# Cross-attention on one core: first context tile in pieces, one DMA request per weight chunk, another written-out order

## The chip, the core and the metric

The kernel runs on one NeuronCore of a Trainium2 chip. Five engines work side by side, each from its own queue in order: TensorE (PE in the profile, with its weight loads as PEld), VectorE (DVE), ScalarE (ACT), GpSimd (POOL) and SyncE (SP), which here only issues DMA requests. Sixteen DMA engines move the data. The metric is the device time of one execution in microseconds (us).

## The reference

Everything is float32. 64 batches of text rows (256 x 512) attend to context rows (256 x 384); hidden size 512:

```python
text_p  = x   @ W_text  + b_text        # (64, 256, 512) @ (512, 512)
audio_p = ctx @ W_audio + b_audio       # (64, 256, 384) @ (384, 512)
Q = layer_norm(text_p,  g1, beta1)
K = layer_norm(audio_p, g2, beta2)
alpha = softmax(Q @ K.T / sqrt(512))
h = alpha @ audio_p                     # V is audio_p
out = layer_norm(h @ W_out + b_out + x, g_out, beta_out)
```

## The kernel before, in words

**Algebra.** The kernel folds W_audio and W_out into one matrix (`fold_multiply`, `wao_sb`), so that the context is weighted directly (`context_*`, `z_part`) and multiplied once. The large products are done by fast schemes that trade multiplications for additions: the projection of q (`Fork`) and the scores take seven block products instead of eight, the projection of k and the output product (`Thirds`) fifteen instead of eighteen. The additions are spread over DVE, POOL and ACT.

**Order.** Nothing is scheduled by a tool while the kernel is built: each engine executes its instructions in the order in which the text calls the methods, and semaphores make a consumer wait for its producer. After the methods' definitions the text has three stretches: first rounds (batches 0 to 2 are started, weights are prepared), a loop `for b in range(3, B - 3)` of 58 rounds in which five batches are in different stages at once (`q2`, `k2` projected, `at` scored, `last` weighted, `old` multiplied out, `settled` normalised), and an end, in which the last batches run out. In each stretch the calls are written in an order worked out by hand or by a planner; the same call set could stand in another order.

**Transfers at the start.** Loads are issued mostly from SP's queue, two early ones from ACT's. A weight matrix lies in SBUF with its rows dealt out in squares: partition q·32 + i holds row (q, k, i) of chunk k. `weight_chunks(t, w, lo, n, queues)` loads chunks lo to lo + n - 1 with four requests, one for each q, each to 32 partitions. The order on SP's queue: the two tiles of the first context batch `c_0`; chunk 0 of the audio weight `wa` (alternating between ACT and SP); chunks 1 and 2 of it; the two tiles of `x_0`; chunks 0 and 1 of the text weight `wt`; the bias row `ba`; chunks 2 and 3 of `wt`; then the second batch's context `cq_1` (`load_c`, four requests by squares, as `load_x`), `bt`, `xq_1`, the output weight `wo`, a bias, and five small requests for `vectors` (`load_vectors`, L163).

**First products.** `keep_busy(6)` runs matmuls on a tile of ones that nothing reads (L187). `RowTurn.tile(t)` turns a tile of batch 0: DVE copies it into squares (`arrange`, L179), PE transposes it chunk by chunk (L202), ACT copies the result out of PSUM (L203). `Projection.multiply(t, chunks)` (L440) then multiplies turned rows by weight chunks: `k[0]` by `wa`, `q[0]` by `wt`, `k[1]` by the centred `wa`. `turn_weights` transposes weight squares (L215); `fold_multiply` (L244) needs `wo`. `means` and `centre` (L272, L279) take the mean off the weights, after which the row means of the projections vanish.

**In the loop.** The output product of a batch, `y`, is a `Thirds`: `y.one()` on PE, `y.copy_n1()` on ACT (L594), `y.start_t()` on DVE (L541), then `y.three()` on PE, which adds to what `start_t` wrote. `Fork.seed()` (ACT) puts the bias where `q3.one()` adds its product. The weights of a batch's softmax go through DRAM to be turned: `at.store_e()`, in the next round `last.fetch_e()`, then `last.turn_e()` on DVE (L76).

**At the end** the last batch's second tile is finished in halves, with two stores of 256 KB at the very end (`store`, L1369, and `store_beside`, L1334).

Of the kernel before, what the change touches and what calls it, by code (L numbers as in the profile page):

```python
# [22 lines left out]
def kernel(  # L23
# [87 lines left out]
    nc.gpsimd.memset(ones, 1.0)  # L111
# [24 lines left out]
    def weight_chunks(t, w, lo, n, queues):  # L136
        v = w.rearrange("(q k i) h -> q i k h", q=NQ, i=SQ)
        for q in range(NQ):
            queues[q].dma_start(t[q * SQ : (q + 1) * SQ, lo : lo + n], v[q, :, lo : lo + n])

    for t in range(ST):
        nc.sync.dma_start(c_0[:, t, :], c_first[:, t, :])
    weight_chunks(wa_sb, w_audio, 0, 1, [nc.scalar, nc.sync, nc.scalar, nc.sync])
    weight_chunks(wa_sb, w_audio, 1, 2, [nc.sync] * NQ)
    for t in range(LT):
        nc.sync.dma_start(x_0[:, t, :], x_first[:, t, :])
# [42 lines left out]
    class RowTurn:  # L189
# [6 lines left out]

        def tile(self, t):
            ar = self.ar[:, t]
            arrange(ar, self.rows[:, t, :], self.chunks, nc.vector.tensor_copy)
            ps = p_at.tile([P, self.chunks, P], F32, tag="at", name="ps_rows")  # L200
            for j in range(self.chunks):
                nc.tensor.transpose(ps[:, j, :], ar[:, j, :], ident)  # L202
            nc.scalar.copy(self.T[:, :, bass.ts(t, P)], ps)  # L203
# [1195 lines left out]

    keep_busy(6)  # L1400
    war = []
    bt_row = bt_sb.rearrange('p (o h) -> p o h', o=1)
    c_turn = RowTurn(c_0, AC, 'cT')
    var_0 = small.tile([P, 4], F32, tag='var4', name='var')
    wa_t = const.tile([P, 11, WP], F32, tag='wa_thirds', name='wa_thirds')
    wao_room = const.tile([P, HC * H], F32, tag='wo', name='wao_thirds')
    pool, tag = (once, 'e')
    c_turn.tile(0)
    k[0] = Projection('k', 0, c_turn.T, wa_sb, ba_sb, AC, ST, bank[0:2])
    war.append(pool.tile([P, HC, P], F32, tag=tag, name=f'war_{0}'))  # L1410
    x_turn = RowTurn(x_0, DC, 'xT')
    c_turn.tile(1)
    k[0].multiply(0, [0])
    pool, tag = (work, 'eT')
    k[0].multiply(1, [0])
    arrange(war[0], wa_sb[:, 0, :], HC, nc.gpsimd.tensor_copy)
    q[0] = Projection('q', 0, x_turn.T, wt_sb, bt_sb, DC, LT, bank[2:4])
    war.append(pool.tile([P, HC, P], F32, tag=tag, name=f'war_{1}'))
    arrange(war[1], wa_sb[:, 1, :], HC, nc.gpsimd.tensor_copy)
    k[0].multiply(1, [1])  # L1420
    mean_wa = means(wa_sb, AC, 'mwa')
    pool, tag = (work, 'eT')
    war.append(pool.tile([P, HC, P], F32, tag=tag, name=f'war_{2}'))
    k[0].multiply(0, [1])
    k[0].multiply(1, [2])
    arrange(war[2], wa_sb[:, 2, :], HC, nc.gpsimd.tensor_copy)
    x_turn.tile(0)
    ba_row = ba_sb.rearrange('p (o h) -> p o h', o=1)
    x_turn.tile(1)
    k[0].multiply(0, [2])  # L1430
    turn_weights(0, 1)
    q[0].multiply(1, [0])
    q[0].multiply(1, [1])
    centre(wa_sb, mean_wa, AC)
    mean_wt = means(wt_sb, DC, 'mwt')
    mean_ba = means(ba_row, 1, 'mba')
    q[0].multiply(0, [0])
    k[0].evict(1)
    k[0].evict(0)
    third_weights(wa_sb, wa_t, [0])  # L1440
    k[0].scales()
    k[0].normalise([1])
    q[0].multiply(0, [1])
    bt_step = const.tile([P, H2], F32, tag='bt_step', name='bt_step')
    mean_bt = means(bt_row, 1, 'mbt')
    cT[1] = turn_c(1)
    k[0].normalise([0])
    q[0].multiply(0, [2])
    q[0].multiply(0, [3])
    turn_weights(1, 1)  # L1450
    turn_weights(2, 1)
    k[1] = Projection('k', 1, cT.pop(1), wa_sb, ba_sb, AC, ST, bank[4:6])
    q[0].multiply(1, [2])
    k[1].multiply(1, [0])
    centre(ba_row, mean_ba, 1)
    k[1].multiply(0, [0])
    turn_weights(3, 1)
    k[1].multiply(1, [1])
    third_weights(wa_sb, wa_t, [2], nc.vector)
    xT[1] = turn_x(1)  # L1460
    q[0].multiply(1, [3])
    k[1].multiply(1, [2])
    k[1].multiply(0, [1])
    k[1].multiply(0, [2])
    fold_multiply(1, 0, 1)
    xs_1 = SumX(xT.pop(1), nc.vector)
    centre(wt_sb, mean_wt, DC)
    centre(bt_row, mean_bt, 1)
    q[0].evict(1)
    g1_sb, be1_sb, g2_sb, be2_sb, bac_sb = take_columns()  # L1470
    wa_blocks = third_weights(wa_sb, wa_t, [3])
    q[0].evict(0)
    wt_blocks = weight_sums(wt_sb, DC // 2, 'wtsum')
    fold_multiply(1, 1, 2)
    k[0].store()
    xs_1.add(1)
    xs_1.add(1)
    load_c(2)
    folds.append(p_at.tile([P, H], F32, tag='at', name='ps_fold'))
    xs[1] = xs_1  # L1480
    k[1].evict(1)
    q[1] = Fork(1, xs.pop(1).of, wt_blocks)
    load_x(2)
    k[1].evict(0)
    xs_1.add(1)
    fold_multiply(1, 2, 3)
    q[0].scales()
    fold_multiply(0, 0, 1)
    third_weights(wa_sb, wa_t, [1], nc.vector)
    part = bias_parts()  # L1490
    load_c(3)
    cT[2] = turn_c(2)
    Fork.seed()
    cs[2] = Sides(cT.pop(2), 'csum')
    q[0].normalise([0])
    cs[2].add(1)
    fold_multiply(2, 0, 1)
    q[1].seven()
    cs[2].add(1)
    cs[2].add(1)  # L1500
    q[1].one()
    nc.vector.tensor_tensor(bt_step, bt_sb[:, :H2], bt_sb[:, H2:], ALU.subtract)
    nc.vector.tensor_scalar(g2_sb, g2_sb, scale, None, ALU.mult)
    q[1].after_seven()
    xT[2] = turn_x(2)
    k[0].fetch()
    q[0].normalise([1])
    nc.vector.tensor_scalar(be2_sb, be2_sb, scale, None, ALU.mult)
    xs[2] = SumX(xT.pop(2))
    xs_1.add(1)  # L1510
    q[0].store()
    fold_multiply(0, 1, 2)
    fold_multiply(0, 2, 3)
    q[1].after_one()
    k[1].square()
    k[1].scales()
    q[1].six()
    q[1].start_q3()
    fold_multiply(0, 3, 4)
    q[1].step_r()  # L1520
    fold_evict(0)
# [3 lines left out]
    load_x(3)  # L1525
    Thirds.seed_with(ba_sb)
    cT[3] = turn_c(3)
    xs[2].add(1)
    cs[2].add(1)
    load_c(4)  # L1530
    bias_rest(part, 1, 2)
    fold_multiply(1, 3, 4)
    xs[2].add(1)
    ba_delta = third_bias(ba_sb, 'ba_delta')
    cs[3] = Sides(cT.pop(3), 'csum')
    k2_0 = k[2] = Thirds('k', 2, cs.pop(2), wa_blocks, ba_sb, ba_delta)
    q[0].fetch()
    q[1].five()
    k2_0.one()
    fold_evict(1)  # L1540
    q[1].after_five()
    xs[2].add(1)
    at_0 = att[0] = Attention(0)
    xs[2].add(1)
    cs[3].add(1)
    k2_0.copy_n1()
    q[2] = Fork(2, xs.pop(2).of, wt_blocks)
    k[1].normalise([0])
    k2_0.two()
    k[1].normalise([1])  # L1550
    at_0.k.turn()
    cs[3].add(1)
    q[1].two()
    third_weights(wa_sb, wa_t, [4], nc.vector)
    q[1].three()
    k2_0.start_t()
    cs[3].add(1)
    q[1].four()
    xT[3] = turn_x(3)
    q[1].square()  # L1560
    k[1].store()
    q[1].scales()
    fold_multiply(2, 1, 2)
    k2_0.three()
    k2_0.copy_t()
    var_2 = small.tile([P, 4], F32, tag='var4', name='var')
    fold_multiply(2, 2, 3)
    q2_0 = q[2]
    k2_0.start_l0()
    k2_0.start_l1()  # L1570
    cs[3].add(1)
    q[1].normalise([0])
    q[1].normalise([1])
    bias_rest(part, 2, 3)
    fold_multiply(2, 3, 4)
    q[1].store()
    cs[3].add(1)
    k2_0.four()
    Fork.seed()
    xs[3] = SumX(xT.pop(3))  # L1580
    cs[3].add(1)
    at_0.affine_keys(0)
    q2_0.one()
    k2_0.take_m()
    bias_rest(part, 3, 4)
    k2_0.start_u()
    q2_0.seven()
    q2_0.after_one()
    xs[3].add(1)
    fold_evict(2)  # L1590
    at_0.affine_keys(3)
    at_0.q.turn()
    load_c_rows(1)
    q2_0.six()
    q2_0.after_seven()
    q2_0.start_q3()
    load_x(4)
    k2_0.five()
    at_0.affine_queries(3)
    xs[3].add(1)  # L1600
    at_0.affine_queries(0)
    q[1].fetch()
    cs[3].add(1)
    k2_1 = k[3] = Thirds('k', 3, cs.pop(3), wa_blocks, ba_sb, ba_delta)
    last_1 = att[0]
    xs[3].add(1)
    k2_0.copy_n()
    k2_0.copy_u()
    xs[3].add(1)
    q[3] = Fork(3, xs.pop(3).of, wt_blocks)  # L1610
    q2_0.step_r()
    q2_0.five()
    k2_0.leave_middle()
    wao_t = wao_room[:, :11 * WP].rearrange('p (n h) -> p n h', n=11)
    at_0.affine_keys(2)
    at_0.affine_keys(1)
    k2_0.middle_d()
    k2_0.leave()
    q2_0.after_five()
    q2_1 = q[3]  # L1620
    fold_bias(part)
    k2_0.square(var_0[:, 2:], [0])
    at_0.score(0, 1)
    k2_0.leave_ends()
    at_0.affine_queries(2)
    q2_0.three()
    at_0.affine_queries(1)
    k2_0.middle_sum()
    k2_0.square(var_0[:, 2:], [1])
    third_weights(wao_sb, wao_t, [1])  # L1630
    q2_0.two()
    k2_0.seed()
    k[1].fetch()
    q2_0.four()
    at_0.score(1, 2)
    load_c(5)
    at_0.score(2, 3)
    q2_0.square(var_0[:, :2], [0])
    at_0.score(3, 4)
    cT[4] = turn_c(4)  # L1640
    q2_0.square(var_0[:, :2], [1])
    var_1 = small.tile([P, 4], F32, tag='var4', name='var')
    xT[4] = turn_x(4)
    scales_of(q2_0, k2_0, var_0)
    at_0.score(4, 5)
    cs[4] = Sides(cT.pop(4), 'csum')
# [829 lines left out]
```

## Time and profile before

| | |
|---|---|
| median of 3 runs | 1337.42 us (1336.81 to 1337.81) |
| profiled execution | 1338.2 us, its span 1336.0 us |
| PE busy | 1328.3 us, 99% of the span, 8495 instructions |
| DVE, ACT, POOL busy | 93%, 87%, 86% |
| granted PE clock | 1.000 |
| DMA queues | q1 (SP) 320.20 MB, 85.8% of 16 engines; q10 (ACT) 0.13 MB |
| HBM | 203.57 MB read, 116.65 MB written |

The span runs from the first to the last instruction of the profiled execution; times in the views are microseconds from the span's start. A busy share is that of one engine over the whole span; a matmul's end is modelled, so that starts of successive matmuls say more than its busy time. In the chain of waits each piece is what released the next one; a row of the timeline gives start, length, engine, line of the kernel, operation, written and read tile, and, in brackets, the idle time before it and who ended it. `x8` behind a row merges eight instructions; a float32 matmul of the text is two PE instructions.

### The profile page before, as it was taken

Reading aid. Unit: us, or ns where it says so; the run is one execution under the profiler, and the core shown is the slowest. Engines: PE = TensorE matmul, PEld = TensorE weight load, DVE = VectorE, ACT = ScalarE, POOL = GpSimd, SP = SyncE. Lnnn points to the kernel's source line nnn. Section 1 sums busy time; section 2 is a strip of 40 time slices with the busy share of each in tenths; the row PEclk is TensorE's granted clock in tenths of the full one; section 3 lists DMA queues with packets and bytes.
Section 4 is the critical chain, followed back from the end, with each engine's and each line's share of the span. In section 5 each row is a group of like instructions: output and inputs, shape, how many; then the busy total and the mean of one; then the engine's idle time right before and its main releaser. Section 6 shows DMA issues by size and latency. Waiting matters only on the chain.

```text
span 1336.0 us, 29959 instructions
## 1 busy us (share of the span) xinstructions
PE 1328.3 (99%) x8495; PEld 1249.6 (94%) x8495; DVE 1243.0 (93%) x3313; ACT 1162.9 (87%) x3310; POOL 1151.5 (86%) x1855
## 2 busy tenths in 40 slices
PE   9999999999999999999999999999999999999998
PEld 5899999999999999999999999999999999999996
DVE  6769999999999999999999999999999999999968
ACT  4898898898898898988988988988889889889885
POOL 5798898898898898988988988988989889889865
PEclk9999999999999999999999999999999999999999
DMA  9988989888888889889888898889988998888773
GB/s 220 243 235 236 242 246 246 242 255 240 251 251 247 245 247 240 259 244 238 255 234 242 253 243 247 243 230 266 254 235 251 255 240 252 246 244 253 209 229 138
DMA packets 448971, 322.24 MB, mean 241 GB/s; under 512 B 153765, under 2 KB 381349, under 8 KB 448806
## 3 DMA queue, kind: packets, MB, share of 16 engines
q1 hardware_dynamic: 448710, 320.20, 85.8%
q8 instruction: 68, 1.11, 0.4%
q14 instruction: 97, 0.79, 0.2%
q10 hardware_dynamic: 96, 0.13, 0.0%
HBM read 203.57 MB, written 116.65 MB: 240 GB/s over the span
## 4 chain that ended last, share of the span: by engine, by line
PE 98%; DMA 1%; ACT 1%; SPq 0%; DVE 0%; issue 0%; DVEq 0%; ACTq 0%
PE ps_f L733 28%; PE ps_m L557 16%; PE ps_sc L884 13%; PE ps_n L557 11%; PE ps_u L557 8%; PE ps_z L1033 7%; PE ps_l L557 5%; PE ps_z L1095 5%; PE ps_sc L823 1%; DMA eq<-ed 1%; PE ps_f L440 0%; PE ps_n L440 0%; PE ps_l L244 0%; PE ps_fold L244 0%; PE ps_u L440 0%; PE ps_m L244 0%
## 5 line engine op out<-in xcount | busy, mean ns | idle before, releaser
L869 POOL TENSOR_TENSOR qsum<-qT 128x256 f32<-128x256 f32 x118 | 112.5, 953 | 101.4 <-ACT qT L527 96.9
L352 POOL TENSOR_TENSOR csum<-csum,cT 128x256 f32<-128x256 f32 x310 | 194.0, 627 | 5.2
L733 PE MATMUL ps_f<-wtsum,xsum 128*128 128x256 f32 x756 | 194.0, 380 | 0.0
L527 ACT ACTIVATE qT<-qT,columns 128x256 f32<-128x256 f32 x256 | 152.2, 597 | 1.8 <-DVE qT L76 1.8
L733 PEld LDWEIGHTS ps_f<-wtsum,xsum 128*128 128x128 f32 x756 | 131.9, 191 | 11.4 <-issue 1.0
L527 ACT ACTIVATE kT<-kT,columns 128x256 f32<-128x256 f32 x256 | 141.2, 609 | 0.0
L733 PE MATMUL ps_f<-wt,xT 128*128 128x256 f32 x504 | 129.5, 379 | 0.0
L884 PE MATMUL ps_sc<-kT,qT 128*128 128x128 f32 x928 | 122.4, 275 | 0.0
L884 PEld LDWEIGHTS ps_sc<-kT,qT 128*128 128x128 f32 x928 | 114.8, 192 | 0.0
L884 PE MATMUL ps_sc<-ksum,qsum 128*128 128x128 f32 x696 | 106.2, 275 | 0.9 <-DVE ps_sc L541 0.9
L1357 DVE SCALAR_TENSOR_TENSOR yr<-yr,rstd,beo 128x512 f32<-128x512 f32 x120 | 106.6, 889 | 0.1
L884 PEld LDWEIGHTS ps_sc<-ksum,qsum 128*128 128x128 f32 x696 | 97.7, 191 | 5.0 <-DVE ps_sc L541 2.2
L733 PEld LDWEIGHTS ps_f<-wt,xT 128*128 128x128 f32 x504 | 91.0, 191 | 9.7
L1348 DVE SCALAR_TENSOR_TENSOR yr<-yr,nm,go 128x512 f32<-128x512 f32 x124 | 95.9, 774 | 0.0
L488 ACT ACTIVATE kr<-kr,rstd 128x512 f32<-128x512 f32 x126 | 92.7, 738 | 0.0
L314 POOL TENSOR_TENSOR xsum<-xT 128x256 f32<-128x256 f32 x124 | 90.6, 732 | 1.9 <-DVE xT L76 1.9
L541 DVE TENSOR_TENSOR ps_l<-ps_m,t 128x171 f32<-128x171 f32 x248 | 83.5, 337 | 7.8 <-ACT t L605 3.3
L1158 ACT ACTIVATE junk<-yr,nm 128x512 f32<-128x512 f32 x124 | 90.2, 727 | 0.3
L794 ACT ACTIVATE junk<-ps_f 128x512 f32<-128x512 f32 x126 | 75.2, 597 | 15.6 <-PE ps_f L733 13.5
L520 DVE STREAM_TRANSPOSE kT<-kq 128x512 f32<-128x512 f32 x122 | 85.3, 701 | 2.9 <-DMA kq<-kd 2.8
L804 ACT ACTIVATE qr<-ps_f,rstd 128x512 f32<-128x512 f32 x126 | 87.8, 699 | 0.1
L1095 PE MATMUL ps_z<-eT,c 128*128 128x256 f32 x296 | 84.6, 380 | 0.0
(302 smaller groups left out, 4653.7 us busy)
## 6 DMA issues: line engine op xcount, KB each, us to landing
kd<-kr SPq DMA_DIRECT2D x64, 512.0 KB, 2.9
kq<-kd SPq DMA_DIRECT2D x256, 128.0 KB, 3.1
qd<-qr SPq DMA_DIRECT2D x64, 512.0 KB, 2.8
qq<-qd SPq DMA_DIRECT2D x256, 128.0 KB, 2.8
xq<-in_x_dram SPq DMA_DIRECT2D x252, 128.0 KB, 3.1
x<-in_x_dram SPq DMA_DIRECT2D x63, 512.0 KB, 5.3
out_dram<-yr SPq DMA_DIRECT2D x62, 512.0 KB, 5.1
cq<-in_ctx_dram SPq DMA_DIRECT2D x252, 96.0 KB, 4.0
```

Source lines behind the costliest of these rows:

```text
L314: self.engine.tensor_tensor(*step)
L352: nc.gpsimd.tensor_tensor(*step)
L488: nc.scalar.mul(row, row, self.r[t])
L527: nc.scalar.activation(self.T[:, k, :], self.T[:, k, :], AF.Identity, bias=bet[:, k : k + 1], scale=gam[:, k : k + 1],)
L557: nc.tensor.matmul(place, lhsT=self.sides.of[n], rhs=self.weights[n], start=(n == 14), stop=True, skip_group_check=True,)
L733: nc.tensor.matmul(place, lhsT=side, rhs=w, start=(n == 7 and c == 0), stop=True, skip_group_check=True,)
L869: nc.gpsimd.tensor_tensor(*self.steps[n])
L884: nc.tensor.matmul(self.place(t, m), lhsT=self.qsides[n][:, c], rhs=self.ksides[n][:, c], start=False, stop=True, skip_group_check=True,)
L1033: nc.tensor.matmul(self.zp[{1: 0, 2: 0, 4: 2}.get(n, 1)], lhsT=self.asides[n], rhs=self.bsides[n], start=(n == 7), stop=True, skip_group_c ...
L1095: nc.tensor.matmul(ps, lhsT=c_rows[self.b][:, s, bass.ts(j, P)], rhs=self.eT[:, s, :], start=start, stop=(s == ST - 1), skip_group_check=True,
L1348: nc.vector.scalar_tensor_tensor(row, row, self.nm[:, t : t + 1], go_sb, ALU.add, ALU.mult)
L1357: nc.vector.scalar_tensor_tensor(self.y[:, t, :], self.y[:, t, :], self.r[t], beo_sb, ALU.mult, ALU.add)
```

## The change

Four things change, beside the order. The tile of ones is written by DVE instead of POOL. `RowTurn.tile` is split into `arrange`, `transpose` and `copy`, each for a range of chunks, and the first context tile is put through in pieces of one and two chunks; all other tiles still go through whole. A weight chunk of 128 partitions is now one request: `weight_chunk(t, w, k, queue)`, whose source is the four blocks of 32 rows of that chunk. Chunk 0 of `wa` is issued on ACT's queue, between the two context tiles; the others on SP's queue. `wo` keeps its four requests (`weight_by_square`).

```diff
-    nc.gpsimd.memset(ones, 1.0)
+    nc.vector.memset(ones, 1.0)
...
-    def weight_chunks(t, w, lo, n, queues):
-        v = w.rearrange("(q k i) h -> q i k h", q=NQ, i=SQ)
-        for q in range(NQ):
-            queues[q].dma_start(t[q * SQ : (q + 1) * SQ, lo : lo + n], v[q, :, lo : lo + n])
-
-    for t in range(ST):
-        nc.sync.dma_start(c_0[:, t, :], c_first[:, t, :])
-    weight_chunks(wa_sb, w_audio, 0, 1, [nc.scalar, nc.sync, nc.scalar, nc.sync])
-    weight_chunks(wa_sb, w_audio, 1, 2, [nc.sync] * NQ)
+    def weight_chunk(t, w, k, queue=nc.sync):
+        queue.dma_start(t[:, k, :], w.rearrange("(q k i) h -> q i k h", q=NQ, i=SQ)[:, :, k])
+
+    nc.sync.dma_start(c_0[:, 0, :], c_first[:, 0, :])
+    weight_chunk(wa_sb, w_audio, 0, nc.scalar)
+    nc.sync.dma_start(c_0[:, 1, :], c_first[:, 1, :])
+    weight_chunk(wa_sb, w_audio, 1)
+    weight_chunk(wa_sb, w_audio, 2)
     for t in range(LT):
         nc.sync.dma_start(x_0[:, t, :], x_first[:, t, :])
-    weight_chunks(wt_sb, w_text, 0, 2, [nc.sync] * NQ)
+    for n in range(2):
+        weight_chunk(wt_sb, w_text, n)
     ba_sb = row(b_audio, "ba")
-    weight_chunks(wt_sb, w_text, 2, 2, [nc.sync] * NQ)
+    for n in range(2, DC):
+        weight_chunk(wt_sb, w_text, n)
...
+        def arrange(self, t, lo, n):
+            j = slice(lo, lo + n)
+            rows = self.rows[:, t, :].rearrange("p (q k i) -> p k q i", q=NQ, i=SQ)
+            nc.vector.tensor_copy(
+                self.ar[:, t, j].rearrange("p k (q i) -> p k q i", q=NQ), rows[:, j]
+            )
+
+        def transpose(self, t, lo, n):
+            self.ps[t, lo] = p_at.tile([P, n, P], F32, tag="at", name="ps_rows")
+            for j in range(n):
+                nc.tensor.transpose(self.ps[t, lo][:, j, :], self.ar[:, t, lo + j, :], ident)
+
+        def copy(self, t, lo, n):
+            nc.scalar.copy(self.T[:, lo : lo + n, bass.ts(t, P)], self.ps[t, lo])
+
         def tile(self, t):
-            ...
+            self.arrange(t, 0, self.chunks)
+            self.transpose(t, 0, self.chunks)
+            self.copy(t, 0, self.chunks)
```

The three stretches keep their set of calls (but for the pieces of the first tile) and get another order. The first rounds now begin so (declarations left out):

```python
    arrange(war[0], wa_sb[:, 0, :], HC, nc.gpsimd.tensor_copy)
    c_turn.arrange(0, 0, 1)
    c_turn.arrange(0, 1, 1)
    keep_busy(6)
    c_turn.transpose(0, 0, 1)
    c_turn.arrange(0, 2, 1)
    c_turn.transpose(0, 1, 2)
    c_turn.copy(0, 0, 1)
    c_turn.arrange(1, 0, 3)
    c_turn.copy(0, 1, 2)
    k[0].multiply(0, [0])
    c_turn.transpose(1, 0, 3)
    c_turn.copy(1, 0, 3)
    k[0].multiply(0, [1])
    k[0].multiply(1, [0])
    k[0].multiply(1, [1])
    x_turn.tile(0)
    k[0].multiply(0, [2])
    k[0].multiply(1, [2])
    x_turn.tile(1)
    q[0].multiply(0, [0])
    turn_weights(0, 1)
    q[0].multiply(0, [1])
    turn_weights(1, 1)
    q[0].multiply(1, [0])
    q[0].multiply(0, [2])
    q[0].multiply(0, [3])
    q[0].multiply(1, [1])
    q[0].multiply(1, [2])
    q[0].multiply(1, [3])
    k[1].multiply(0, [0])
```

In the loop PE's order changes little: of its 32 calls, score part 6 moves ahead of `q2.two` and `y.one`, `z_part(7)` ahead of `y.two`, `z_part(1)` ahead of score part 2, `q3.one` ahead of `z_part(5)`, and the two halves of `context_two` stand together. On the other queues: `Fork.seed` moves behind both exponentials, `add_c21` ahead of `turn_c`, `k.turn([1])` and `turn_e` change places with neighbours, `load_x_rows` and `load_c_rows` move to the places of later stores and fetches on SP, and `fetch_e` comes behind the first additions of the round in the text, still ahead of the next loads on SP. In the end the order changes throughout; the very last calls are now `settle_beside`, `store_beside(0)`, `settle_half` twice and `store(1, 1)`.

More of the change, by code (lines that the diff above doesn't have):

```diff
@@ L1480 @@
[L1480 to L1501, printed above, removed]
@@ L1591 @@
[L1591 to L1612, printed above, removed]
@@ L1768 @@
[L1768 to L1787 removed]
+    q2_1.square(var_1[:, :2], [1])
+    k[2].fetch()
+    k2_2.two()
@@ L2318 @@
[L2318 to L2337 removed]
+    k2_m3.fetch()
```

1539 lines of the change are left out of this document (786 added, 753 removed).

## The prediction

> **What bounds the kernel now.** I read the busy shares first, then the chain that ended last, then tables by stage, then TensorE's own timeline.
>
> ```profile
> span 1336.0 us, 29959 instructions
> PE 1328.3 (99%) x8495; PEld 1249.6 (94%) x8495; DVE 1243.0 (93%) x3313; ACT 1162.9 (87%) x3310; POOL 1151.5 (86%) x1855
> PE 98%; DMA 1%; ACT 1%; SPq 0%; DVE 0%; issue 0%; DVEq 0%; ACTq 0%
> ...
> 139.09 0.89 PE ps_sc L884 x8
> 143.75 1.73 PE ps_f L733 x8
> ...
> 159.39 0.89 PE ps_sc L884 x8
> ...
> 161.28 0.74 PE L557 MATMUL ps_m<-wa_thirds,csum 128*128 128x171 f32 x4
> 161.85 0.74 PE L557 MATMUL ps_l<-wa_thirds,cT 128*128 128x171 f32 x4
> ...
> 140.00:160.00 20.00, 20.00 (x133) 19.17 (x133) 19.31 (x53) 18.08 (x52) 17.80 (x29) 1.00 0.89 251
> ```
>
> PE (TensorE) is the bound, and 98% of the chain is PE. A round of the loop takes 159.39 - 139.09 = 20.30 us in the chain of waits. A busy PE need not be a full one, so I counted. From start to start a matmul instruction takes 0.89 / 8 = 0.111 us at 128 columns, (161.85 - 161.28) / 4 = 0.145 at 171, 1.73 / 8 = 0.216 at 256, and 0.43 at 512 (the eight of 14.79, below, are followed at 18.22). A round issues 28 of 256 (projection of q), 60 of 171 (projection of k and the output), 42 of 128 (scores and context) and 4 of 256 (context): 6.05 + 8.70 + 4.66 + 0.86 = 20.27 us. The round has no idle PE worth naming. DVE (VectorE), 19.31 of 20 us busy, has the least to spare.
>
> So time can only be won ahead of the first matmul, behind the last, or in single hiccups. The start:
>
> ```profile
> 1.56 2.93 PE L187 MATMUL ps_f<-ones 128*128 128x128 f32 x12 [1.56 <-POOL ones L111]
> 4.54 1.63 PE L202 MATMUL ps_rows<-ident,cTr 128*128 128x128 f32 x6
> 6.01 1.73 PE L440 MATMUL ps_m<-wa,cT 128*128 128x512 f32 x2
> ...
> 13.07 1.88 PE L440 MATMUL ps_n<-wt,xT 128*128 128x512 f32 x4
> 14.79 3.60 PE L440 MATMUL ps_u<-wt,xT 128*128 128x512 f32 x8
> 18.22 0.82 PE L215 MATMUL ps_wa<-ident,war 128*128 128x128 f32 x6
> 18.88 1.02 PE L440 MATMUL ps_n<-wt,xT 128*128 128x512 f32 x2
> 19.74 1.88 PE L440 MATMUL ps_f<-wa,cT 128*128 128x512 f32 x4
> ```
>
> The first matmul of the first projection starts at 6.01; each row starts where the one before leaves off, 0.43 us to an instruction of 512 columns. This stage lives on transfers arriving just in time:
>
> ```profile
> DMA  0039988689999999999999999999999707998899
> GB/s 0 0 63 360 305 206 276 167 224 292 325 301 238 213 213 265 246 238 203 216 234 221 288 232 240 251 213 202 213 238 204 121 3 268 350 247 213 233 246 240
> DMA packets 7114, 6.61 MB, mean 220 GB/s; under 512 B 2818, under 2 KB 4937, under 8 KB 7114
> ...
> POOL war L179 <- DMA wa<-in_L_xattn_W_audio_dram: 5.5, 2, 3.7
> DVE cT L76 <- DMA cq<-in_ctx_dram: 0.4, 1, 0.4
> ACT junk L272 <- DMA wt<-in_L_xattn_W_text_dram: 0.2, 1, 0.2
> ```
>
> That is 0 to 30 us in 40 slices of 0.75. All sixteen DMA engines are about nine tenths busy from 2.25 us on. The best slice moves 360 GB/s, the mean is 220.
>
> **The change, part by part.** The sum is made against the profiled execution: 1338.2 us with its span of 1336.0, which is 0.8 above the median of 1337.42 shown. All instructions of the three stretches (first rounds, loop, end) are the same set, permuted, apart from the first context tile's pieces. So PE's own work, the floor, does not move.
>
> *One request per chunk.* Before, a weight goes in requests of 32 partitions each, four to a chunk or to a pair of chunks:
>
> ```profile
> 1.63 3.35 SPq L139 DMA_DIRECT2D wa<-in_L_xattn_W_audio_dram  x6
> 5.02 0.90 SPq L146 DMA_DIRECT2D x<-in_x_dram  x2
> 5.96 1.84 SPq L139 DMA_DIRECT2D wt<-in_L_xattn_W_text_dram  x4
> 8.31 2.32 SPq L139 DMA_DIRECT2D wt<-in_L_xattn_W_text_dram  x4
> ```
>
> The SP queue issues fourteen weight requests in 3.35 + 1.84 + 2.32 = 7.5 us; after, it issues six, so what stands behind them (x_0, bias, cq_1, w_out) is issued some 4 us sooner. That alone buys little, as the engines are already full. What matters is the shape. The source of a chunk is now three-dimensional, four blocks of 32 rows with a jump between blocks, and the destination is 128 partitions. Whether such a request is dealt to all sixteen engines, by its 128 rows, or to four, by its four blocks, no row of before shows at this size. Nearest are the five small requests for the vectors, whose source steps over four blocks too:
>
> ```profile
> 19.02 0.25 SPq L163 DMA_DIRECT2D vectors<-in_L_xattn_g_dram  x1
> ...
> 22.67 0.25 SPq L163 DMA_DIRECT2D vectors<-in_L_xattn_b_audio_dram  x1
> 24.06 0.40 SPq L498 DMA_DIRECT2D kd<-kr  x1
> ...
> 23.90:24.20 0.30, 0.30 (x2) 0.19 (x1) 0.30 (x2) 0.00 (x0) 0.01 (x1) 1.00 0.13 23
> 2.25:3.00 0.75, 0.75 (x6) 0.75 (x5) 0.00 (x0) 0.00 (x0) 0.00 (x0) 1.00 0.99 360
> ```
>
> (The last two columns are the busy share of the sixteen engines and GB/s.) The last of the five is issued at 22.67; a microsecond later, with nothing else issued until 24.06, the share is 0.13, where a queue that feeds all engines shows 0.99. A share under 4/16 is what four engines give; rows so small could also simply be done early, so it is weak evidence. The two ends are: sixteen engines, no loss; four engines at the mean rate, 220 x 4/16 = 55 GB/s. I take four engines at the best slice's rate, 360 x 4/16 = 90 GB/s, since that slice is what an engine is seen to reach, and the row nearest in pattern points to four.
>
> The Trainium skill (DMA: Bandwidth & Descriptors, "Why a DMA increments its semaphore by 16 and not by 1", how many engines) says that a request is split along the slowest dimension of both access patterns, over the largest count up to 16 that divides both. By that rule four blocks against 128 partitions give four, and the low share above agrees with it. The same page puts an engine at about 27 GiB/s; as an estimate from that page, four would carry 116 GB/s and the last chunk of the text weight would land near 20.6 us, a loss of 3.8 us instead of the one below.
>
> The cost at 90 GB/s. Seven chunks of 0.262 MB all pass the same four engines: 1.835 MB. Ahead of or between them go c_0, x_0 and one bias, 1.18 MB, a quarter of which falls to these engines: 0.295 MB. Together 2.13 MB / 90 GB/s = 23.7 us, from the first moved bytes at 2.2: the fourth text chunk lands at 25.9. PE needs it for `q[0].multiply(0, [3])`; with that one, four pairs of 512-column instructions, 4 x 0.86 = 3.44 us, stand before the first matmul of `k[1]`: 29.3. In before `k[1]` starts at 19.74, with one pair of q (0.86) still to come and three transposes (0.33) already done, so the same state of work is at 20.27. Loss: 29.3 - 20.3 = 9.1 us. What is late next is not binding: cq_1 (0.39 MB, a quarter on these engines) lands 1.1 us behind the text chunk, ahead of 29.3; w_out follows bt, xq_1 and itself, 1.83 MB, 0.46 on the four, 5 us: 32.5, and the fold that reads it comes 2 x 2.57 + 0.67 us behind 29.3, at 35.1. As PE has no slack afterwards, the 9.1 us stay to the end.
>
> *First tile in pieces, ones by VectorE.* The tile's chain is DVE copy, three transposes, ACT copy:
>
> ```profile
> 3.94 0.55 DVE L179 COPY cTr<-c 128x384 f32<-128x384 f32 x1 [2.95 <-DMA c<-in_ctx_dram]
> 4.54 0.50 PEld L202 LDWEIGHTS ps_rows<-ident,cTr 128*128 128x128 f32 x3 [0.35 <-DVE cTr L179]
> 5.48 0.48 ACT L203 COPY cT<-ps_rows 128x384 f32<-128x384 f32 x1 [3.49 <-PE ps_rows L202]
> ```
>
> A third of it first: 0.2 + 0.25 + 0.25 instead of 0.55 + 0.73 + 0.48, about 1.0 us sooner, and the three transposes of the second tile (0.33) now stand behind the first matmul instead of ahead: a gain of 0.7 if the audio chunk is there. With four engines it is not: 0.262 MB and the interleaved context land at about 2.2 + (0.262 x 2) / 90 = 8.0, so this step is worth 0. The ones by DVE start the idle matmuls of L187 about 0.45 us sooner; the first real work waits for data, so 0 as well.
>
> *Loop order.* PE's order is nearly the old one. The distances that shrink: `y.one` to `y.three` has 1.31 us of PE work between (a product of q, one score part) instead of 1.75, to cover this copy and this subtraction:
>
> ```profile
> 166.63 0.28 ACT L594 COPY n<-ps_n 128x171 f32<-128x171 f32 x1
> ...
> 167.12 0.33 DVE L541 TENSOR_TENSOR ps_u<-ps_n,n 128x171 f32<-128x171 f32 x1
> ```
>
> 0.61 us, with one more ACT square (0.63) ahead in the queue: 1.24, just inside. `Fork.seed` moves behind both exponentials, but `q3.one` is not due for half a microsecond. `last.fetch_e` is issued earlier and `turn_e` keeps its place. I take 0; a stall of 0.05 us a round would cost 58 x 0.05 = 2.9.
>
> *End.*
>
> ```profile
> 1329.91 1.02 PE L1286 MATMUL ps_f<-beo,ident 128*128 128x512 f32 x2
> ...
> 1332.33 0.35 SPq L1369 DMA_DIRECT2D out_dram<-y  x1
> 1332.78 0.37 SPq L1334 DMA_DIRECT2D out_dram<-w  x1
> ```
>
> The two last stores trade places, both of 256 KB, behind the same DVE work: -0.1.
>
> Sum: 1338.2 + 9.1 + 0 + 0 - 0.1 = 1347.2; less the 0.8 between the profile and the median, 1346.4.
>
> **The rivals.**
>
> *Not slower: all sixteen engines.* The place is the seven weight requests, the price is the whole 9.1. It decides at the rate at which the fourth text chunk is there when PE wants it: without a wait `q[0].multiply(0, [3])` would stand at 20.3 - 3.4 - 0.7 (the front's gain) = 16.2 us, so 2.13 MB in 14.0 us, 152 GB/s on those engines; any more and nothing is lost. For it: fewer, larger requests leave SP idle sooner, and four of sixteen would be a poor way to deal 128 rows. Against it: the 0.13 above. Then the front gains 0.7 and the rest nothing: 1337.4 - 0.7 = 1336.7.
>
> *Four engines, slow.* At 55 GB/s the chunk lands at 2.2 + 38.7 = 40.9, 24 us late: 1361. For it: the mean of the first 30 us, and later requests for all engines compete for memory. Against: few engines run, and 360 is in the slices.
>
> *A wait in the loop.* DVE has 0.7 us to spare in a round; a piece of it lost to a late `copy_n1` or `turn_e` would show as a longer round. At 0.1 us a round, 5.8 us: 1343 with sixteen engines. For it: DVE at 19.31 of 20. Against: the distances above.
>
> **How the numbers follow.** 0.2% is 2.7 us, about what a measurement of this kernel can tell from no change. Four engines near the best slice (1343 to 1349): 0.56. Four engines, slower: 0.12. Sixteen engines: 0.27, of which 0.02 beyond 0.2% faster. A wait in the loop by itself: 0.05, mostly slower. Faster 0.02, same 0.26, slower 0.72. The likeliest gives 1346.4, its own range 1343 to 1349. The range that holds 8 in 10 must take in the sixteen-engine case: 1336.0 to 1350.0, leaving out 0.12 above and a little below.
>
> **What would show it.** In the changed profile: the busy share of the DMA engines from 3 to 20 us well under a half, near 0.3 to 0.5 instead of 0.9; the landing of a weight chunk several times that of the context tile; PE idle in front of L440 with the text weight as releaser; `k[1]`'s first matmul near 29; the round still 20.30. The prediction is wrong if the share stays at 0.9 and L440 starts near 5; then the time is 1336.7. A round of 20.35 or more would mean that the order, not the requests, costs.

## The result, and the profile after

The changed kernel takes 1351.02 us (median of four runs, 1350.07 to 1351.90) against 1337.38 for the kernel before: a ratio of 1.0101 (95% interval 1.0089 to 1.0114), 13.6 us slower. The prediction was 1346.4 with 1336.0 to 1350.0 around it: the sign and the mechanism came as forecast, the size did not.

First the page of the changed kernel (its span, busy shares, and the engines' shares of the chain that ended last), then the transfers of its first 30 us in 40 slices of 0.75 us:

```profile
span 1349.3 us, 29701 instructions
PE 1334.2 (99%) x8495; PEld 1248.2 (93%) x8495; DVE 1256.6 (93%) x3316; ACT 1173.8 (87%) x3311; POOL 1172.4 (87%) x1854
...
PE 97%; DMA 2%; SPq 0%; DVE 0%; issue 0%; DVEq 0%
```

```profile
DMA  0049425995222473222222226353654368943239
GB/s 0 0 61 352 143 83 147 332 213 131 98 98 98 156 249 137 98 101 96 104 98 98 98 109 162 121 150 114 156 144 118 120 254 244 217 77 73 83 113 248
DMA packets 3799, 4.12 MB, mean 137 GB/s; under 512 B 1259, under 2 KB 2390, under 8 KB 3799
```

Before, nearly every slice from 2.25 us on stood at 9. Now slice after slice shows a busy share of two tenths and the same rate, 98 GB/s: four of sixteen engines at work (4/16 = 0.25), each at 98 / 4 = 24.5 GB/s. (From 15 to 17.25 us, a stretch with weights alone, the share is 0.26.) The slices between them, up to 352 GB/s, are those in which other requests go along: context, text and bias rows, and from about 18 us on those of the next batch.

TensorE's timeline of the changed kernel (start, length, engine, line, operation; in brackets the idle time before and what ended it; L455 is the former L440):

```profile
1.04 2.93 PE L188 MATMUL ps_f<-ones 128*128 128x128 f32 x12 [1.04 <-DVE ones L111]
3.76 0.85 PE L210 MATMUL ps_rows<-ident,cTr 128*128 128x128 f32 x3
8.28 2.05 PE L455 MATMUL ps_m<-wa,cT 128*128 128x512 f32 x2 [3.67 <-DMA wa<-in_L_xattn_W_audio_dram]
...
20.56 1.13 PE L455 MATMUL ps_u<-wt,xT 128*128 128x512 f32 x2 [1.62 <-DMA wt<-in_L_xattn_W_text_dram]
...
24.19 1.13 PE L455 MATMUL ps_u<-wt,xT 128*128 128x512 f32 x2 [1.31 <-DMA wt<-in_L_xattn_W_text_dram]
28.04 2.07 PE L455 MATMUL ps_u<-wt,xT 128*128 128x512 f32 x2 [2.72 <-DMA wt<-in_L_xattn_W_text_dram]
29.90 4.72 PE L455 MATMUL ps_n<-wt,xT 128*128 128x512 f32 x6
34.45 2.74 PE L455 MATMUL ps_f<-wa,cT 128*128 128x512 f32 x6
...
1343.65 1.02 PE L1301 MATMUL ps_f<-beo,ident 128*128 128x512 f32 x2
```

TensorE waits for the first audio chunk (3.67 us) and then for three text chunks. `k[1]` starts at 34.45; the same state of work stood at 20.27 before. That is +14.2 us. From there to the last matmul row it takes 1343.65 - 34.45 = 1309.2 us, before 1329.91 - 20.27 = 1309.6; behind that row 5.65 us, before 6.09. So 14.18 - 0.44 - 0.44 = 13.3, the difference of the two spans: the whole loss lies ahead of `k[1]`.

A second thing stands in these rows. The pair at 24.19 takes 1.13 us, the one at 28.04 2.07: half the pace. Windows of the same kernel (bounds, length, PE, PEld, DVE, ACT, POOL busy, granted PE clock, share of the DMA engines, GB/s):

```profile
24.00:28.00 4.00, 1.13 (x2) 0.30 (x2) 1.44 (x6) 1.38 (x4) 1.50 (x4) 0.88 0.62 167
28.00:30.00 2.00, 1.96 (x3) 0.93 (x4) 0.81 (x1) 0.72 (x2) 0.00 (x0) 0.50 0.58 157
30.00:32.00 2.00, 2.00 (x4) 0.91 (x3) 0.63 (x3) 1.49 (x4) 0.00 (x0) 0.50 1.04 238
32.00:34.00 2.00, 2.00 (x3) 0.67 (x2) 0.78 (x2) 0.64 (x1) 1.27 (x1) 0.53 1.05 216
34.00:36.00 2.00, 2.00 (x6) 0.95 (x5) 1.39 (x4) 0.00 (x0) 0.66 (x1) 1.00 0.57 107
```

The granted clock is 0.50 from 28 to 32 and 0.53 to 34. The four pairs that the prediction put at 3.44 us take 34.45 - 28.04 = 6.4. The prediction has no term for this. The pace was halved once before, behind the wait of 3.67 us: the pair at 8.28 takes 2.05 us. There it costs nothing, as TensorE waits for text chunks afterwards. The column of the granted clock does not show it: from 7.5 to 9 us it reads 1.00, so in these first microseconds only the matmuls themselves tell the pace.

The steady rounds are untouched. In the chain of waits of the changed kernel:

```profile
133.59 0.89 PE ps_sc L899 x8
...
153.89 0.89 PE ps_sc L899 x8
```

153.89 - 133.59 = 20.30 us, the round of before.

### The profile page after: what moved, and what is told of

It is laid out like the page before. It is cut to its first block, busy times and chain, and to the rows that moved or that the text cites. A ratio compares the mean times of both kernels' runs of the same rounds, so it can differ in the third digit from the quotient of the medians.

```text
span 1349.3 us, 29701 instructions
## 1 busy us (share of the span) xinstructions
PE 1334.2 (99%) x8495; PEld 1248.2 (93%) x8495; DVE 1256.6 (93%) x3316; ACT 1173.8 (87%) x3311; POOL 1172.4 (87%) x1854
## 4 chain that ended last, share of the span: by engine, by line
PE 97%; DMA 2%; SPq 0%; DVE 0%; issue 0%; DVEq 0%
PE ps_f L748 28%; PE ps_m L572 16%; PE ps_sc L899 13%; PE ps_n L572 11%; PE ps_u L572 8%; PE ps_z L1048 7%; PE ps_l L572 5%; PE ps_z L1110 5%; PE ps_sc L838 1%; DMA wt<-in_L_xattn_W_text_dram 1%; DMA wa<-in_L_xattn_W_audio_dram 1%; PE ps_f L455 0%; PE ps_n L455 0%; PE ps_l L259 0%; PE ps_fold L259 0%; PE ps_m L259 0%
## 5 line engine op out<-in xcount | busy, mean ns | idle before, releaser
L367 POOL TENSOR_TENSOR csum<-csum,cT 128x256 f32<-128x256 f32 x310 | 202.6, 654 | 0.5
L884 POOL TENSOR_TENSOR qsum<-qT 128x256 f32<-128x256 f32 x118 | 86.1, 730 | 59.5 <-ACT qT L542 57.0
L542 ACT ACTIVATE kT<-kT,columns 128x256 f32<-128x256 f32 x256 | 134.0, 595 | 0.6 <-DVE kT L76 0.6
L899 PE MATMUL ps_sc<-kT,qT 128*128 128x128 f32 x928 | 131.8, 275 | 0.0
L1372 DVE SCALAR_TENSOR_TENSOR yr<-yr,rstd,beo 128x512 f32<-128x512 f32 x120 | 123.8, 1032 | 0.0
L899 PEld LDWEIGHTS ps_sc<-kT,qT 128*128 128x128 f32 x928 | 121.2, 191 | 0.0
L1363 DVE SCALAR_TENSOR_TENSOR yr<-yr,nm,go 128x512 f32<-128x512 f32 x124 | 109.9, 887 | 0.5 <-ACT junk L1173 0.5
L503 ACT ACTIVATE kr<-kr,rstd 128x512 f32<-128x512 f32 x126 | 84.6, 727 | 0.0
L475 ACT ACTIVATE junk<-kr 128x512 f32<-128x512 f32 x126 | 80.9, 642 | 0.2
L76 DVE STREAM_TRANSPOSE qT<-qq 128x1024 f32<-128x1024 f32 x64 | 78.7, 1229 | 1.9 <-DMA qq<-qd 1.8
```

The costliest lines, as they stand in the source:

```text
L367: nc.gpsimd.tensor_tensor(*step)
L542: nc.scalar.activation(self.T[:, k, :], self.T[:, k, :], AF.Identity, bias=bet[:, k : k + 1], scale=gam[:, k : k + 1],)
L884: nc.gpsimd.tensor_tensor(*self.steps[n])
L899: nc.tensor.matmul(self.place(t, m), lhsT=self.qsides[n][:, c], rhs=self.ksides[n][:, c], start=False, stop=True, skip_group_check=True,)
L1363: nc.vector.scalar_tensor_tensor(row, row, self.nm[:, t : t + 1], go_sb, ALU.add, ALU.mult)
L1372: nc.vector.scalar_tensor_tensor(self.y[:, t, :], self.y[:, t, :], self.r[t], beo_sb, ALU.mult, ALU.add)
```

## The experiments

The theory: the loss is the weight requests alone, because a source of four blocks is carried by four engines; a late transfer and a clock halved by the idle time it leaves make up the 14 us. Rivals: the new order or the pieces carry part of it; the requests are slow for another reason than the number of blocks; the half clock is a by-product without a price.

**The requests undone.** The changed kernel with the four-square requests of before:

```diff
-    def weight_chunk(t, w, k, queue=nc.sync):
-        queue.dma_start(t[:, k, :], w.rearrange("(q k i) h -> q i k h", q=NQ, i=SQ)[:, :, k])
+    def weight_chunks(t, w, lo, n, queues):
+        v = w.rearrange("(q k i) h -> q i k h", q=NQ, i=SQ)
+        for q in range(NQ):
+            queues[q].dma_start(t[q * SQ : (q + 1) * SQ, lo : lo + n], v[q, :, lo : lo + n])
...
+    weight_chunks(wa_sb, w_audio, 0, 1, [nc.scalar, nc.sync, nc.scalar, nc.sync])
...
```

> The changed kernel, with the weight requests of before (four requests of 32 partitions for a chunk or a pair of chunks, in before's order of issue); pieces, ones by VectorE and all three orders stay. Theory (the requests run on four of the sixteen DMA engines, and the wait for them and the half clock that it brings are the whole loss): the loss goes; 1336.4 to 1337.2, the fourth text chunk is there before TensorE wants it, the clock is never granted at half behind 10 us, DMA share about 0.9 from 3 to 20 us. Rival (the new order of the first rounds, the loop or the end costs): some of the 13.6 us stays, 1340 or more.

Measured: 1339.13 us, ratio 1.0012 (1.0002 to 1.0021). Some 12 of the 13.6 us are gone with the requests; 1.8 are left, more than the theory allowed (1336.4 to 1337.2) and less than its rival (1340 or more). Three later runs come back to them.

**The requests alone.** The kernel before, with one request per chunk, and the old order, tile and ones:

```diff
-    weight_chunks(wa_sb, w_audio, 0, 1, [nc.scalar, nc.sync, nc.scalar, nc.sync])
-    weight_chunks(wa_sb, w_audio, 1, 2, [nc.sync] * NQ)
+    weight_chunk(wa_sb, w_audio, 0, nc.scalar)
...
+    weight_chunk(wa_sb, w_audio, 1)
+    weight_chunk(wa_sb, w_audio, 2)
...
```

> The kernel before, with the weight requests of the changed kernel alone (one per chunk, same order of issue); order, whole first tile and ones by GpSimd as before. Theory (four engines): nearly the whole loss appears, 1348 to 1353, about 98 GB/s over long stretches, TensorE waits for the text weight. Rival (orders): within 3 us of 1337.4.

Measured: 1350.31 us, ratio 1.0097 (1.0083 to 1.0111). By themselves the requests bring 13.0 of the 13.6 us. With the run before, which took them away, this shows from both sides that the loss is theirs. TensorE's waits for the text weight and the start of `k[1]`, in the fastest of the four executions (1348.80):

```profile
21.07 2.08 PE L441 MATMUL ps_n<-wt,xT 128*128 128x512 f32 x2 [2.20 <-DMA wt<-in_L_xattn_W_text_dram]
27.77 1.13 PE L441 MATMUL ps_u<-wt,xT 128*128 128x512 f32 x2 [1.35 <-DMA wt<-in_L_xattn_W_text_dram]
30.25 1.88 PE L441 MATMUL ps_f<-wa,cT 128*128 128x512 f32 x4
```

`k[1]` is 30.25 - 19.74 = 10.5 us late, as against the same order before. In the old order the half pace (2.08 us) stands behind the first of these waits, and behind the second the pace is full again: the slow stretch does not fall at the same place in both kernels.

**Four blocks, none, two.** The next two change only the source's shape. One request per chunk over 128 rows that lie in one piece:

```diff
-        queue.dma_start(t[:, k, :], w.rearrange("(q k i) h -> q i k h", q=NQ, i=SQ)[:, :, k])
+        queue.dma_start(t[:, k, :], w.rearrange("(k p) h -> p k h", p=P)[:, k])
```

> The changed kernel, but a chunk's one request reads 128 rows that lie on end in DRAM instead of four blocks of 32 rows; same bytes, same number of requests, same row length and queue. The weight rows sit in other partitions than the products suppose, so what is computed is not the reference; no time depends on values. Theory (four blocks, four engines): 128 rows are dealt to all sixteen engines, the loss goes: 1336.2 to 1337.2, share near 0.9 in the first 20 us. Rival (one large request of 256 KB is slow as such, or SP's queue is held by it): stays near 1351.

Two requests per chunk, each with a source of two blocks:

```diff
-        queue.dma_start(t[:, k, :], w.rearrange("(q k i) h -> q i k h", q=NQ, i=SQ)[:, :, k])
+        v = w.rearrange("(q k i) h -> q i k h", q=NQ, i=SQ)[:, :, k]
+        for q in (0, 2):
+            queue.dma_start(t[q * SQ : (q + 2) * SQ, k, :], v[q : q + 2])
```

> The changed kernel, but each chunk goes in two requests of 64 partitions, each with a source of two blocks. Theory (as many engines as blocks, and the same ones for all requests): two engines carry all weights, about 49 GB/s instead of 98 in the stretches with weights alone, the fourth text chunk lands near 2.2 + 2 x 25.7 = 54 us less what the context and x share was, say 46 to 54, and the time is 1370 to 1382. Rival (size of a request): smaller requests help, 1340 to 1349. A middle one (two requests run on different pairs of engines): unchanged, 1351.

Measured: 1336.67 us, ratio 0.9995 (0.9986 to 1.0004), for the 128 rows in one piece; 1367.76, ratio 1.0228 (1.0209 to 1.0246), for two blocks. The transfers of the first 30 us, first of the one, then of the other:

```profile
DMA  0068999999999999999999999995108999888897
GB/s 0 0 139 272 405 351 325 336 350 380 393 243 224 382 352 236 254 242 230 206 251 262 198 199 229 221 198 100 30 0 333 317 262 212 192 203 213 201 298 197
```

```profile
DMA  0059311111111111697111111111111115411111
GB/s 0 0 174 263 104 44 32 53 48 55 49 49 55 49 49 49 208 325 205 44 49 49 49 52 49 49 49 49 49 49 49 49 52 221 167 55 52 49 49 49
```

The same bytes to the same 128 partitions: up to 405 GB/s from 128 rows, 98 from four blocks, 49 from two. So 49 / 2 = 98 / 4 = 24.5 GB/s an engine, and 405 / 16 = 25.3: with two and with four blocks the number of blocks is the number of engines, with 128 rows all sixteen work. This agrees with the rule of the Trainium skill (DMA: Bandwidth & Descriptors, "Why a DMA increments its semaphore by 16 and not by 1") that the prediction weighed. As the first of the two runs keeps the size and the number of the requests, neither of these is the reason. The two-block case came 2 us under its forecast of 1370 to 1382; its direction and its rate are clear. The case of 128 rows meets the prediction's rival of sixteen engines in its number, 1336.7 forecast and 1336.67 measured; that it does so to a few hundredths is luck, since the interval runs from 1.9 us faster than before to 0.5 slower.

**The half clock priced.** The changed kernel with matmuls on the ones where TensorE waits for the text chunks; nothing reads them:

```diff
+    keep_busy(6)
     q[0].multiply(0, [1])
...
+    keep_busy(5)
     q[0].multiply(0, [2])
+    keep_busy(11)
     q[0].multiply(0, [3])
```

> The changed kernel, with idle matmuls (the ones matrix, as in the warm-up) added where TensorE waits for text chunks: six ahead of q[0](0,[1]), five ahead of q[0](0,[2]), eleven ahead of q[0](0,[3]). The transfers are as in the changed kernel. Theory: beside the late landing (27.95 us) the half clock from 27.3 to 34.1 us costs 3.0 us of its own, because TensorE idled between the chunks. With fillers the clock stays full, four pairs take 3.4 us instead of 6.4, k[1] starts near 31.5 instead of 34.45, and the time is about 1348.0. Rival: the half clock does not come from the idle gaps or costs nothing that is not given back later: the rows between 28 and 34 stay at half speed, or the time stays at 1350.5 to 1351.5.

Measured: 1348.37 us (1347.70 to 1349.35, all below the lowest run of the changed kernel, 1350.07), ratio 1.0081 (1.0065 to 1.0096). TensorE's timeline and two windows of it:

```profile
25.01 2.62 PE L188 MATMUL ps_f<-ones 128*128 128x128 f32 x22
27.70 1.12 PE L455 MATMUL ps_u<-wt,xT 128*128 128x512 f32 x2
28.66 2.74 PE L455 MATMUL ps_n<-wt,xT 128*128 128x512 f32 x6
31.23 2.74 PE L455 MATMUL ps_f<-wa,cT 128*128 128x512 f32 x6
```

```profile
24.00:28.00 4.00, 3.88 (x25) 3.21 (x26) 1.38 (x5) 1.56 (x5) 1.50 (x4) 1.00 0.63 164
28.00:30.00 2.00, 2.00 (x6) 0.81 (x5) 0.90 (x1) 0.46 (x2) 0.00 (x0) 1.00 0.77 184
```

The chunk is there 0.34 us earlier (27.70 against 28.04), the clock stays at 1.00, and the four pairs take 31.23 - 27.70 = 3.5 us instead of 6.4. So 2.9 us of the loss were the clock, by this row; by the medians the fillers bring 2.65 (1351.02 - 1348.37), 0.3 of which may be the earlier chunk. Work that does nothing makes the changed kernel faster.

**Part of the weights.** The audio weight by squares, the text weight by one request per chunk:

```diff
-    weight_chunk(wa_sb, w_audio, 0, nc.scalar)
     nc.sync.dma_start(c_0[:, 1, :], c_first[:, 1, :])
-    weight_chunk(wa_sb, w_audio, 1)
-    weight_chunk(wa_sb, w_audio, 2)
+    weight_chunks(wa_sb, w_audio, 0, 1, [nc.scalar, nc.sync, nc.scalar, nc.sync])
+    weight_chunks(wa_sb, w_audio, 1, 2, [nc.sync] * NQ)
```

> The changed kernel, but the audio weight goes by the four-square requests of before; only the four chunks of the text weight are one request each. Theory: it is the sum of bytes on the four engines that sets the landing: four text chunks, 1.05 MB, and a quarter of what goes between, some 0.4 to 0.5 MB, at 83 GB/s: the fourth lands near 20 to 21 us, TensorE waits for it where it stood at 16 to 17 us, loss 4 to 5 us and up to 2 more if the clock drops: 1341 to 1344. Rival: the audio chunk, first in the line, carries the loss, and the text weight alone is hidden: 1338 to 1339.5, no wait with the text weight as releaser.

Measured: 1344.85 us, ratio 1.0052 (1.0039 to 1.0066). The rival, that the audio chunks alone carry the loss, is out: 7.4 us of it come with the text weight alone. The theory has the sign, and its range ends 0.85 us too low. Timeline and window:

```profile
22.95 1.12 PE L459 MATMUL ps_u<-wt,xT 128*128 128x512 f32 x2 [2.53 <-DMA wt<-in_L_xattn_W_text_dram]
23.91 4.43 PE L459 MATMUL ps_n<-wt,xT 128*128 128x512 f32 x6
28.18 2.74 PE L459 MATMUL ps_f<-wa,cT 128*128 128x512 f32 x6
```

```profile
24.00:26.00 2.00, 2.00 (x4) 0.85 (x3) 1.50 (x3) 0.67 (x3) 0.00 (x0) 0.50 0.96 225
```

The fourth chunk is there at 22.9, not at 20 to 21, and the clock halves here too, at about 24, behind an idle stretch of 2.53 us. Dividing bytes by one mean rate does not place a landing to 2 us.

**What the order, the pieces and the ones are worth.** With the squares, the first tile whole again, both tiles turned ahead of the first projection, and the ones by GpSimd, only the changed order of first rounds, loop and end is left:

```diff
-    nc.vector.memset(ones, 1.0)
+    nc.gpsimd.memset(ones, 1.0)
...
-    weight_chunk(wa_sb, w_audio, 0, nc.scalar)
...
+    weight_chunks(wa_sb, w_audio, 0, 1, [nc.scalar, nc.sync, nc.scalar, nc.sync])
...
-    c_turn.arrange(0, 0, 1)
-    c_turn.arrange(0, 1, 1)
     keep_busy(6)
-    c_turn.transpose(0, 0, 1)
...
+    c_turn.tile(0)
+    c_turn.tile(1)
```

> Four-square requests for both weights, the first context tile whole again, both tiles turned ahead of the first projection, ones by GpSimd: the front of before under the changed kernel's order of first rounds, loop and end. Theory: the pieces opened the gap in which the clock stayed at half, so this gives about 1337.3, within 0.5 of before, with the first projection near 6.0 and the clock full at about 7.5. Rival: the order of the first rounds, loop or end costs 1 to 2 us by itself: 1338.5 to 1339.5.

Measured: 1337.31 us, ratio 0.9998 (0.9989 to 1.0007). Taken together, the three orders cost and bring nothing that can be told. That points to the pieces and the ones for the 1.8 us left with the squares, but does not show it: the two intervals (1.0002 to 1.0021, 0.9989 to 1.0007) overlap, and the run with 128 rows had pieces and ones too, at 1336.67. What the timelines show, first with the squares and pieces, then with the squares and whole tiles:

```profile
4.26 0.87 PE L209 MATMUL ps_rows<-ident,cTr 128*128 128x128 f32 x3 [0.30 <-DVE cTr L202]
5.49 2.04 PE L454 MATMUL ps_m<-wa,cT 128*128 128x512 f32 x2 [0.35 <-DMA wa<-in_L_xattn_W_audio_dram]
...
8.06 1.50 PE L454 MATMUL ps_m<-wa,cT 128*128 128x512 f32 x2
...
21.23 2.74 PE L454 MATMUL ps_f<-wa,cT 128*128 128x512 f32 x6
```

```profile
4.49 1.57 PE L209 MATMUL ps_rows<-ident,cTr 128*128 128x128 f32 x6
5.96 3.13 PE L454 MATMUL ps_m<-wa,cT 128*128 128x512 f32 x4
8.93 1.88 PE L454 MATMUL ps_l<-wa,cT 128*128 128x512 f32 x4
...
20.77 2.74 PE L454 MATMUL ps_f<-wa,cT 128*128 128x512 f32 x6
```

With the pieces the first projection starts 0.47 us sooner, behind two gaps of 0.30 and 0.35 us, and its pairs run at half pace (2.04 us) or partly so (1.50) past 8 us. With whole tiles there is no gap and `k[1]` is 0.46 sooner; but there too the first four matmuls take 8.93 - 5.96 = 2.97 us to the next row, where full pace takes 1.72. So the gaps are not needed for the half pace, and `k[1]` accounts for 0.46 of the 1.8 us.

To see whether the gaps were it, they were filled, and the second context tile was issued behind the first audio chunk:

```diff
-    for t in range(ST):
-        nc.sync.dma_start(c_0[:, t, :], c_first[:, t, :])
+    nc.sync.dma_start(c_0[:, 0, :], c_first[:, 0, :])
     weight_chunks(wa_sb, w_audio, 0, 1, [nc.scalar, nc.sync, nc.scalar, nc.sync])
+    nc.sync.dma_start(c_0[:, 1, :], c_first[:, 1, :])
...
-    keep_busy(6)
+    keep_busy(7)
...
     c_turn.transpose(0, 1, 2)
+    keep_busy(1)
```

> Four-square requests for both weights, the second context tile issued behind the first audio chunk, one idle matmul more in the warm-up and one more between the transposes and the first projection; all else as in the changed kernel. Theory: what the squares leave over (1339.1 against 1337.3) is mostly the clock: two gaps of TensorE, 0.30 and 0.35 us, held it at half until 9.1 us instead of 7.5. With the gaps filled and the chunk sooner the clock is full by 5.5 to 7.5, k[1] starts at 19.2 to 20.2 instead of 21.23, the time is 1336.8 to 1338.0. Rival: the loop's or the end's new order carries the 1.8 us: the start improves but the time stays at 1338.5 to 1339.5.

Measured: 1338.22 us, ratio 1.0004 (0.9995 to 1.0013); between the theory's range and the rival's, and 0.9 below the squares with pieces. But `k[1]` starts at 21.56, later than there (21.23) and not at the 19.2 to 20.2 of the theory. TensorE's timeline, and one piece of the chain of waits up to 40 us:

```profile
5.21 1.02 PE L454 MATMUL ps_m<-wa,cT 128*128 128x512 f32 x2
...
8.79 1.10 PE L454 MATMUL ps_m<-wa,cT 128*128 128x512 f32 x2 [1.84 <-ACT junk L286]
...
21.56 2.74 PE L454 MATMUL ps_f<-wa,cT 128*128 128x512 f32 x6
```

```profile
4.26 4.33 DMA wa<-in_L_xattn_W_audio_dram
```

The first half of the theory holds: the first pair now takes 1.02 us, full pace, at 5.21. The second does not: TensorE arrives earlier at the second audio chunk, whose last request lands at 4.26 + 4.33 = 8.59, and waits 1.84 us for it. (The row names ACT's `junk`, which reads the audio weight for the means, a call that the list of the first rounds leaves out; its pass over this chunk starts at 8.74, so both most likely waited for the transfer.) With the pieces alone that chunk was there by 8.06, where its matmul did not wait, so in this execution it also came half a microsecond later; whether the changed order of issue did that, no run shows. As `k[1]` is later here and the median lower, the start of `k[1]` in one execution does not account for differences of 1 us between medians, and what the 1.8 us were stays open.

Last, the version that the runs pointed to: whole tiles, no gap, full pace early, and both products of the first audio chunk ahead of the second:

```diff
-    nc.gpsimd.memset(ones, 1.0)
+    nc.vector.memset(ones, 1.0)
...
-    keep_busy(6)
+    keep_busy(7)
...
-    k[0].multiply(0, [1])
     k[0].multiply(1, [0])
+    k[0].multiply(0, [1])
```

> The kernel of e8 (four-square requests, whole context tiles turned ahead of the first projection) with the ones by VectorE, one idle matmul more in the warm-up, and the second half of the first projection taken ahead of the second chunk of its first half, so that both products of the first audio chunk stand ahead of the wait for the second. Theory: TensorE busy from 1.04 us without a gap is at its full pace by about 5.1, as in the squares with fillers, where in e8 it came some 2.5 us later; the first projection starts at 5.5 to 5.8 and k[1] at 19.6 to 20.2 instead of 20.77: 1336.2 to 1336.9. Rival: the second audio chunk, landing at 8.0 or later behind sixteen busy engines, is what sets k[1]; the early start only makes the wait longer: 1337.0 to 1337.8.

Measured: 1337.29 us, ratio 0.9998 (0.9989 to 1.0007): the rival's time. Its timeline:

```profile
5.79 1.12 PE L454 MATMUL ps_m<-wa,cT 128*128 128x512 f32 x2
6.75 1.02 PE L454 MATMUL ps_l<-wa,cT 128*128 128x512 f32 x2
7.89 1.10 PE L454 MATMUL ps_m<-wa,cT 128*128 128x512 f32 x2
...
12.94 1.10 PE L454 MATMUL ps_u<-wt,xT 128*128 128x512 f32 x2 [0.49 <-DMA wt<-in_L_xattn_W_text_dram]
...
20.54 2.74 PE L454 MATMUL ps_f<-wa,cT 128*128 128x512 f32 x6
```

At full pace from 5.79 on, TensorE reaches the second audio chunk about when it is there (7.89, where 6.75 + 0.86 = 7.61 would be no wait at all). It then waits 0.49 us for the first text chunk and has `k[1]` 0.23 us sooner than with whole tiles alone. So the rival's time holds, but the wait is mostly a later one than it named: here the faster TensorE only met the next transfer. No version beats the kernel before by more than can be told.

## Why the prediction was wrong in size

*One request per chunk, four engines: right.* The step that decided the sign held: a busy share of 0.43 from 3 to 20 us (0.3 to 0.5 forecast) and of 0.26 when weights go alone, three waits with the text weight as releaser, the round at 20.30. The requests alone bring nearly the whole loss, and the shape of their source decides it. The first audio chunk is used at 8.28 (8.0 forecast), in part by luck: the sum put 0.262 MB of context beside it, of which these engines carry a quarter, while its second 0.262 MB was in fact the next audio chunk, under way on the other queue and landing at 10.6.

*The landing of the fourth text chunk: 2.1 us short.* Forecast 25.9, its matmul at 28.04. 2.13 MB in 28.0 - 2.2 = 25.8 us is 83 GB/s where the term took 90. The engine's own rate was not too high: alone, four carry 98. At 98 the 1.835 MB of weights take 18.7 us, which leaves 7.1 us for everything else; the term had 0.295 / 90 = 3.3, a quarter of c_0, x_0 and the bias. Part of the rest can be placed. Between the third and the fourth text chunk no other request stands in SP's queue, and yet their matmuls start 28.04 - 24.19 = 3.85 us apart, where 0.262 MB at 98 GB/s take 2.7. In that stretch the slices rise to 254 GB/s: `cq_1`, `bt` and `xq_1`, issued from 14.79 on, were under way. The prediction named such requests in its slow rival ("later requests for all engines compete for memory") and gave them no term in the sum. That they slowed the chunk is argued from the times; no run took them away.

*Four pairs at full pace: 3.0 us short.* This is the step that failed most: "four pairs of 512-column instructions, 4 x 0.86 = 3.44 us". The prediction forecast idle time in front of L440 and priced the matmuls behind it as if TensorE had never stopped. They took 6.4 us at a granted clock of 0.50, and the fillers show that the idle time caused it and that it is worth 2.65 to 2.9 us. A row that the prediction shows had the sign of it: the first pair of the first projection, at 6.01, is followed at 7.58, 1.57 us for two instructions, where the prediction read 0.43 us for each. With both terms, 9.1 + 2.1 + 3.0 = 14.2, the shift of `k[1]`. The Trainium skill (TensorE: Matmul & The Clock Gate, "HAM oscillation — how this bites in real kernels") warns of idle gaps of more than about 3.4 us; the longest gap of this stretch was 2.72, and in the run with the text weight alone in one piece 2.53, so the measurement goes further than the page: in the window from 24 to 28 TensorE was busy 1.13 of 4 us, and that was enough.

*SP's later requests "some 4 us sooner": wrong, at no cost.* Two views of the SP queue, the changed kernel first, then before:

```profile
14.79 6.67 SPq L73 DMA_DIRECT2D cq<-in_ctx_dram  x4
23.25 5.57 SPq L73 DMA_DIRECT2D xq<-in_x_dram  x4
```

```profile
10.90 2.47 SPq L73 DMA_DIRECT2D cq<-in_ctx_dram  x4
14.15 1.92 SPq L73 DMA_DIRECT2D xq<-in_x_dram  x4
```

With fewer requests ahead of it, `xq_1` was issued 9 us later. The rows merge issuing and waiting between requests. One request of `cq_1` took 1.22 to 2.48 us to issue, before 0.31; one of `xq_1` took no longer than before (0.31 to 0.45 in both), but between them SP waited 3.9 us for text chunks to land. As the prediction found the fold's loads not binding, nothing more was lost.

*Pieces and ones at 0: right in the changed kernel,* where TensorE waits 3.67 us for the chunk behind them. The 0.7 us gain claimed for sixteen engines agrees with 128 rows in one piece (0.7, interval -0.5 to 1.9, so that no gain is possible too), but not with the squares.

*Loop at 0: right,* 20.30. *End at -0.1:* 0.44 us behind the last matmul row, and 0.4 more between `k[1]` and that row; small, and in the right direction.

*The range.* It ended at 1350.0, since it held four engines near one rate as one case and left everything slower to a case at 1361. The two terms that were too small add to the same side, and together they carried the time 1.0 us past the end of the range.

## What to carry to other kernels

Fewer requests are not cheaper requests: look at the outermost dimension of both sides of a transfer, as here four blocks into 128 partitions used four engines of sixteen, and a busy share that stands at a constant 0.26 (with two blocks 0.13) was the sign of it. When a step puts idle time in front of TensorE, price the matmuls behind it at half pace for some microseconds as well, unless they end in another wait that hides it. Look for it in the time from one matmul's start to the next and in the granted clock, not in the busy share, which read 99% before and after. In the last two runs, with all DMA engines already full, making TensorE ready sooner only changed which transfer it waited for.

## What the runs showed of the hardware

- A request over a source of four blocks moved 98 GB/s, over two blocks 49, over 128 rows up to 405: 24.5 to 25.3 GB/s for each engine in use.
- An idle stretch of 2.72 us behind two shorter ones (1.62 and 1.31) brought the granted clock to 0.50 from about 27 to 34 us; with 44 matmul instructions on the ones in the three waits, 22 of them in the longest, it stayed at 1.00.
- In the first microseconds the granted clock read 1.00 (7.5 to 9 us) while a pair of matmuls took 2.05 us, twice its time at full pace.
- While requests of four blocks were under way, SP needed 1.22 to 2.48 us to issue one `cq_1` request, before 0.31, and waited for landings between others: a slow transfer held up the requests behind it.
